# A four-layer Trainium2 kernel: the mixer's filters and first inputs made beside attention 2, its later inputs in steps

## The chip, the cores and the metric

The kernel runs on one core of one Trainium2 chip. A core has five engines that matter here, each working through its own instructions in order: PE (matrix products, with weight loads shown as PEld), DVE (vector operations), ACT (activations), POOL (a second vector engine) and SP (issues DMAs). The engines wait for each other through semaphores. The metric is the device time of one execution in microseconds (us); the time of a kernel is the median of its runs.

## The reference

Everything is float32. The input x has 2 images of 56 x 56 positions (L = 3136) and C = 128 channels. The stages are chained: two layers of selective scans with their convolutions and gates, then attention 2, then the mixer (a spectral layer), attention 3, and a layer of experts. What the change touches is the mixer and the two attentions around it. Attention 2 is self-attention of each position over all others but itself, with a residual. The mixer takes u, the layer-normalized tokens, and computes

```python
# phi: (length, K=16) filters; M_plus, M_minus: (4, K, d, d); sgn = +1, -1, +1, ...
Vf = rfft(phi, n); Uf_p = rfft(u, n); Uf_m = rfft(u * sgn, n)
U_plus = irfft(Vf * Uf_p)[:sl]            # causal convolution of every channel with 16 filters
U_minus = irfft(Vf * Uf_m)[:sl] * sgn
s = sigma ** 0.25
out = einsum('btkd,k,kde->bte', U_plus, s, Mpp) + einsum('btkd,k,kde->bte', U_minus, s, Mpm)
out += sum(shift(u, i) @ Mu[i] for i in range(3))      # the "direct" part
```

The four sets of matrices hold for four stretches of the sequence, weighted by a softmax over log_weights + gumbel.

## The kernel before

**Order of the stages.** `program` (L2179) runs the two scan layers, then inside attention 2's memory `MixerInputs` (L1511) and `Attention2.run` (L1297), then `Attention3.__init__` (L1322), `layer2_mixer` (L1801), attention 3 and the experts. A scheduler that knows dependences orders the instructions of each engine from the order in which the code issues them; on the chip each engine keeps that order. Memory that a pool gives back is waited for by the next pool that gets it.

**Filters.** `mixer_filters` (L1460) runs first in `Attention2.run`. POOL clears P (32 x 1712), a DMA loads the filters of 16 indices and two parities into it, and another stores them to DRAM as `raw`. For four sets A, B, C and D of blocks, DVE makes the filter at seven points (-1, 1, -2, 2, half, 0, inf): the convolution of 4 blocks by 4 blocks is done as 7 products of block polynomials at points, in place of 16. Of these, 88 DVE steps work on 32 partitions; four DMAs store the sets to `win`, and 32 DMAs copy `raw` to `last`, the taps of the last rows. The pool m2f holds all this, and it is given back before attention 2's pools open.

**Attention 2** (`Attend.run`, L1203). Of 14 chunks (2 images by 7) of 448 queries each has 25 key tiles. A key tile is a product sc on PE (L1224), an Exp on ACT into one of six buffers e (L1226), a mask by DVE where keys meet their own queries (L1231), a running total on POOL (L1237), and a product av on PE (L1218). Between the tiles the hook `also(at, j)` makes the mixer's inputs of the chunk before: tokens, channels, blocks (into x, which has 13 blocks of 128 positions of one parity) and the direct part (L1600), which needs `wu`, sums of Mu by the weights. The tail of layer 1 before it (L1034 to L1066) and `Attention2.chunk` (L1281, with L1293 and key_tiles L1433) make the normalized tokens, transposed, in seven steps.

**The mixer** has 32 units: 2 parities of the input (`pin`), 8 pairs of filters (f0), 2 parities of the filter (eo). Units 0 to 15 have pin 0. A unit has four squares; a square makes products at seven points on PE (`product`, L1703), which DVE and ACT evict and interpolate (L1725 to L1739), and POOL completes by two additions (L1741). The squares are T by A (u0), A by A plus T by B in one (u2), C by C (S), D by D (u1). Their results are added (L1761, L1772), and `project` (L1842) multiplies them with matrices and DVE adds to A (L1848). For eo = 0 there is also the `remainder` (L1788). Six PSUM banks hold products. The right sides are windows of `win` (`windows`, L1691 and on, through DMAs on SP).

**Values.** The left sides of the products are the input at the seven points, v["T"], v["A"], v["C"], v["D"]: `Mixer.inputs` (L1630). Their input comes from POOL and ACT (L1643 to L1650), and ten DVE steps make the values (L1655 to L1664), all issued in one go. T and A are made ahead of unit 0 and again at the end of unit 15 (inside `coming`); C and D within units 0 and 16, ahead of the squares that need them. `fetch` (L1624) loads the odd parity of x ahead of unit 15. The first windows of all sets, taps and matrices are loaded in `layer2_mixer` ahead of the loop; `Attention3.__init__` (L1338 to L1351) multiplies its weights into one matrix, on PE, ahead of all of these.

Of the kernel before, what the change touches and what calls it, by code (L numbers as in the profile page):

```python
# [14 lines left out]
F32 = mybir.dt.float32  # L15
# [6 lines left out]
B = 2  # L22
HW = 56
L = HW * HW
C = 128
# [1240 lines left out]
class Attention2:  # L1266
# [30 lines left out]
    def run(self, early, inputs):  # L1297

        k = self.k
        done = early()  # L1300
        with k.pool("a2") as sp, ExitStack() as ctx:
            skip = sp.tile([KT, KT], F32, name="skip")
            k.nc.vector.tensor_scalar(skip, k.ident, -1.0, 1.0, ALU.mult, ALU.add)
            att = Attend(k, ctx)

            def also(at, j):
                steps = {4: inputs.tokens, 11: inputs.channels, 14: inputs.blocks, 18: inputs.direct}
                if at > 0 and j in steps:
                    steps[j](lambda: att.bank("lo"), *divmod(at - 1, NCH))

            att.run(self.uT, self.uT, self.V, 128.0**-0.5, k.ident, skip=skip, also=also)
            for step in (inputs.tokens, inputs.channels, inputs.blocks, inputs.direct):
                step(lambda: att.bank("lo"), B - 1, NCH - 1)
        return done


class Attention3:
# [4 lines left out]
    def __init__(self, k, ctx, d):  # L1322
# [11 lines left out]
        with k.pool("pa3w", psum=True) as pp:  # L1334
            turned = {}
            for n in ("Wq", "Wk"):
                ps = bank(pp, n)[:, 0:C]
                nc.tensor.transpose(ps, W[n], k.ident)  # L1338
                turned[n] = wp.tile([C, C], F32, name=n)
                nc.vector.tensor_copy(turned[n], ps)  # L1340
            ps = bank(pp, "Wq")[:, 0:C]
            nc.tensor.matmul(ps, lhsT=turned["Wq"], rhs=turned["Wk"], start=True, stop=True)
            nc.vector.tensor_copy(self.weights, ps)
            ps = bank(pp, "Wk")[:, 0:1]
            nc.tensor.matmul(ps, lhsT=turned["Wk"], rhs=W["bq"], start=True, stop=False)
            nc.tensor.matmul(ps, lhsT=self.weights, rhs=less[:, 0:1], start=False, stop=True)
            nc.vector.tensor_copy(self.c, ps)
            ps = bank(pp, "Wq")[:TP, 0:C]
            nc.tensor.matmul(ps, lhsT=less, rhs=W["Wv"], start=True, stop=False)
            nc.tensor.matmul(ps, lhsT=k.ones[:, :TP], rhs=W["bv"], start=False, stop=True)  # L1350
            nc.vector.tensor_copy(self.bias, ps)  # L1351
# [102 lines left out]
POINTS = ("-1", "1", "-2", "2", "half", "0", "inf")  # L1454
# [5 lines left out]
def mixer_filters(k, d, dp):  # L1460
# [3 lines left out]
    raw = dp.tile([32, PW], F32, name="raw")  # L1464
    win = dp.tile([32, NWIN, WIDE], F32, name="win")
    last = dp.tile([32, KB, NB + 1, REST], F32, name="last")
    with k.tc.tile_pool(name="m2f", bufs=1) as fp:
        P = fp.tile([32, PW], F32, name="P")
        nc.gpsimd.memset(P, 0.0)
        nc.sync.dma_start(P[:, KB - TP : KB + HL], d["L2_phi"].rearrange("f p m -> (f p) m"))  # L1470
        nc.sync.dma_start(raw, P)
        v = nc.vector
        for g, bases in enumerate(SETS.values()):
            D = fp.tile([32, len(POINTS), WIDE], F32, name=f"D{g % 2}")
            h = [P[:, KB * (bases[0] + i) + 1 : KB * (bases[0] + i) + 1 + WIDE] for i in range(4)]
            if len(bases) > 1:
                both = fp.tile([32, 4, WIDE], F32, name="both")
                for i in range(4):
                    at = KB * (bases[1] + i) + 1
                    v.tensor_tensor(both[:, i], h[i], P[:, at : at + WIDE], ALU.add)  # L1480
                h = [both[:, i] for i in range(4)]
            even, odd = (fp.tile([32, WIDE], F32, name=n) for n in ("even", "odd"))
            for p, (m1, m2) in enumerate(((1 / 9, -1 / 3), (-1 / 60, 1 / 36))):
                v.scalar_tensor_tensor(even, h[2], float(4**p), h[0], ALU.mult, ALU.add)
                v.scalar_tensor_tensor(odd, h[3], float(4**p), h[1], ALU.mult, ALU.add)
                v.tensor_scalar_mul(odd, odd, float(2**p))
                for q, (m, op) in enumerate(((m1, ALU.subtract), (m2, ALU.add))):
                    v.tensor_tensor(D[:, 2 * p + q], even, odd, op)
                    v.tensor_scalar_mul(D[:, 2 * p + q], D[:, 2 * p + q], m)
            v.scalar_tensor_tensor(even, h[1], 0.5, h[0], ALU.mult, ALU.add)  # L1490
            v.scalar_tensor_tensor(odd, h[3], 0.5, h[2], ALU.mult, ALU.add)
            v.scalar_tensor_tensor(even, odd, 0.25, even, ALU.mult, ALU.add)
            v.tensor_scalar_mul(D[:, 4], even, 32 / 45)
            v.tensor_scalar_mul(D[:, 5], h[0], -0.5)
            v.tensor_copy(D[:, 6], h[3])
            nc.sync.dma_start(win[:, len(POINTS) * g : len(POINTS) * (g + 1)], D)
# [4 lines left out]
    return last, win  # L1501


class MixerInputs:
# [6 lines left out]
    def __init__(self, k, ctx, early, d, A, uT):  # L1511
# [44 lines left out]
        mu = ep.tile([128, 4, 3, C], F32, name="mu")  # L1556
        nc.sync.dma_start(mu, d["L2_M_u"].rearrange("i s d e -> d i s e"))
        self.wu = ep.tile([128, 4, 3, C], F32, name="wu")
        stretch_sums(nc.vector, self.wu, mu, lambda i: wt[:, i : i + 1])

# [46 lines left out]
class Mixer:  # L1607
# [5 lines left out]
    def __init__(self, k, ctx, given, last, win):  # L1613
        self.k, self.x, self.odd, self.last, self.win = k, given.x, given.odd, last, win
# [7 lines left out]
        self.W, self.v, self.waiting = {}, {}, []  # L1622
# [7 lines left out]
    def inputs(self, name):  # L1630


        nc, x = self.k.nc, self.x
        n = B * C

        def at(t, i0, m):
            return t[:, i0 : i0 + m]

        if name == "C":
            c = x[:, 4:11]  # L1640
        else:
            c = self.scratch("u0" if name == "D" else "u1", 7)
            if name == "T":  # L1643
                nc.scalar.copy(at(c, 0, 4), x[:, 8:12])
                nc.gpsimd.memset(at(c, 4, 3), 0.0)
            elif name == "A":
                nc.gpsimd.tensor_tensor(c, x[:, 0:7], x[:, 4:11], ALU.subtract)
            else:
                nc.gpsimd.tensor_tensor(at(c, 0, 4), x[:, 8:12], x[:, 4:8], ALU.subtract)
                nc.scalar.activation(at(c, 4, 3), x[:, 8:11], AF.Copy, scale=-1.0)  # L1650
        v = self.sp.tile([KB, len(POINTS), n], F32, name="v" + name)
        e = at(v, 0, 6)
        f, g = self.scratch("T4", 4), self.scratch("T", 2)
        stt, tt = nc.vector.scalar_tensor_tensor, nc.vector.tensor_tensor
        stt(e, at(c, 0, 6), -0.5, at(c, 1, 6), ALU.mult, ALU.add)  # L1655
        stt(f, at(e, 0, 4), -4.0, at(e, 2, 4), ALU.mult, ALU.add)
        tt(g, at(e, 3, 2), at(e, 1, 2), ALU.subtract)
        tt(v[:, 0], f[:, 2], f[:, 1], ALU.subtract)
        tt(v[:, 1], f[:, 2], f[:, 1], ALU.add)
        stt(v[:, 2], g[:, 0], -2.0, g[:, 1], ALU.mult, ALU.add)  # L1660
        stt(v[:, 3], g[:, 0], 2.0, g[:, 1], ALU.mult, ALU.add)
        stt(v[:, 4], c[:, 3], -5.0, c[:, 5], ALU.mult, ALU.add)
        stt(v[:, 4], c[:, 1], 4.0, v[:, 4], ALU.mult, ALU.add)
        tt(at(v, 5, 2), at(f, 2, 2), at(f, 0, 2), ALU.subtract)  # L1664
        self.v[name] = v

    def scratch(self, name, n):
        if name[0] == "T":
            t = self.half(name)
        else:  # L1670
            t = self.block(name)
        t = t.rearrange("p b f c -> p (b f c)")
        return t[:, 0 : n * B * C].rearrange("p (k c) -> p k c", c=B * C)
# [15 lines left out]
    def windows(self, name, f0, eo):  # L1689
        n, n0 = len(POINTS), len(POINTS) * list(SETS).index(name)  # L1690
        t = self.wp.tile([KB, 2, n, KB], F32, name="w" + name)  # L1691
        for f in range(2):
            r = (2 * (f0 + f) + eo) * NWIN + n0
            self.k.nc.sync.dma_start(
                t[:, f], bass.AP(self.win.tensor, self.win.offset + r * WIDE, [[1, KB], [WIDE, n], [1, KB]])
            )
# [12 lines left out]
    def square(self, u, *pairs):  # L1709
# [23 lines left out]
        ps = self.product(4, pairs)  # L1733
        for o, share in ((t(0), -0.25), (t(1), -0.125), (y(2), 1.25), (y(1), 0.625)):
            stt(o, ps, share, o, ALU.mult, ALU.add)  # L1735
        T4 = self.half("T4")
        nc.scalar.activation(T4, T, AF.Copy, scale=4.0)  # L1737
        tt(y(0), self.product(5, pairs), y(2), ALU.add)
        tt(y(3), self.product(6, pairs), y(1), ALU.add)  # L1739
# [3 lines left out]
    def unit(self, f0, eo, after, later, project, ready, coming):  # L1743

        nc = self.k.nc
        u0 = self.block("u0")
        self.square(u0, ("T", "A"))
        self.finish(1)
        u2 = self.block("u2")
# [5 lines left out]
        if ready:  # L1755
            self.inputs("C")
# [468 lines left out]
```

## Time and profile before

| | us |
|---|---|
| median of 3 runs (8737.68, 8746.86, 8752.1) | 8746.86 |
| profiled execution | 8761.79 |
| its span | 8760.0 |
| layers 0 and 1, to the last scan product | 0 to 5532 |
| tail of layer 1 and preparation of attention 2 | 5532 to 5650 |
| filters | 5650 to 5676 |
| attention 2 | 5676 to 6295 |
| mixer | 6295 to 7869 |
| attention 3 | 7869 to 8560 |
| experts, to the end | 8560 to 8760 |

The granted clock is 0.964 in the mean. The profile is one execution on the chip; its times are microseconds from the start of the span. A row of the timeline gives the start, the duration, the engine, the line of the kernel, the operation, the tiles it writes and reads, how many were run in a row (x), and in brackets the idle time of the engine just before, with what ended it. A row of the windows view gives the busy time of each engine within a stretch. A busy time says little by itself: a step matters where another engine that sets the end stands idle for it.

### The profile page before, as it was taken

The page shows a single profiled execution, that of the slowest core. Times are in us where ns is not written, and L with a number is a line of the kernel's source. Part 1 is how long each engine was busy: PE and PEld are TensorE (multiplying, and loading weights), DVE is VectorE, ACT ScalarE, POOL GpSimd, SP SyncE. Part 2 cuts the span into 40 slices and gives each one's busy share as a digit, 9 for nine tenths or more (in the row PEclk, how much of TensorE's full clock was granted, in tenths as well). Part 3 has the DMA queues.
Part 4 walks back from the last instruction along what each step waited for, and adds up shares of the span by engine and source line. Part 5 has one row for each costly group of instructions (what it writes and reads, how often), then busy time and mean ns, then how long its engine had stood idle before and what let it go on. Part 6 is the DMA issues. An engine that isn't in the chain of part 4 may idle for free. (4 is left out here: it accounts for less than half of the span.)

```text
span 8760.0 us, 106320 instructions
## 1 busy us (share of the span) xinstructions
PE 8013.3 (91%) x32199; PEld 4929.5 (56%) x32199; DVE 6642.9 (76%) x6889; ACT 5622.6 (64%) x12956; POOL 6845.1 (78%) x4232
## 2 busy tenths in 40 slices
PE   8999999999998898898888889699899989989998
PEld 4555555555555454445444455355488878865555
DVE  8999998999996997998899799711266676665442
ACT  6888876888876997998898799543322222224330
POOL 5999986999995997998899799566667767756551
PEclk9999999999998999999999999799999999989999
DMA  5666663666663884886788598300133433310004
GB/s 147 217 217 210 211 194 115 217 218 214 211 199 96 228 224 127 218 224 165 183 230 219 130 232 223 80 14 4 47 97 102 116 87 101 102 47 8 15 1 140
DMA packets 846633, 1276.86 MB, mean 146 GB/s; under 512 B 182813, under 2 KB 504350, under 8 KB 846058
## 3 DMA queue, kind: packets, MB, share of 16 engines
q1 hardware_dynamic: 846058, 1270.07, 51.8%
q8 instruction: 254, 4.16, 0.2%
q14 instruction: 321, 2.63, 0.1%
HBM read 1230.00 MB, written 46.58 MB: 146 GB/s over the span
## 5 line engine op out<-in xcount | busy, mean ns | idle before, releaser
L495 POOL TENSOR_TENSOR p<-h,c 128x784 f32<-128x784 f32 x2048 | 3765.8, 1867 | 209.2 <-DVE h L401 114.0
L401 DVE TENSOR_TENSOR_SCAN h<-a,state,h 128x784 f32<-128x784 f32 x1104 | 1993.7, 1834 | 29.5 <-POOL h L498 27.2
L421 PE MATMUL acc<-p,center 128*128 128x392 f32 x4096 | 1482.7, 500 | 24.3 <-POOL p L495 24.2
L421 PE MATMUL acc<-p,ident 128*128 128x392 f32 x4096 | 1427.8, 492 | 0.5 <-POOL p L495 0.4
L479 DVE TENSOR_TENSOR h<-du,b 128x784 f32<-128x784 f32 x1024 | 976.9, 954 | 192.5 <-PE b L407 175.5
L421 PEld LDWEIGHTS acc<-p,center 128*128 128x128 f32 x4096 | 747.6, 192 | 546.6 <-POOL p L495 57.2
L421 PEld LDWEIGHTS acc<-p,ident 128*128 128x128 f32 x4096 | 746.5, 190 | 532.4 <-issue 29.5
L1237 POOL TENSOR_TENSOR total<-total,e 128x448 f32<-128x448 f32 (+1 forms) x644 | 735.6, 1142 | 328.7 <-ACT e L1226 289.4
L1226 ACT ACTIVATE e<-sc 128x448 f32<-128x448 f32 (+1 forms) x700 | 377.5, 543 | 723.2 <-PE sc L1224 594.6
L498 POOL TENSOR_TENSOR h<-du,b 128x784 f32<-128x784 f32 x448 | 832.8, 1859 | 0.0
L381 ACT ACTIVATE a<-delta,L1A 128x784 f32<-128x784 f32 x768 | 700.9, 913 | 148.3 <-DVE h L401 144.2
L401 DVE TENSOR_TENSOR_SCAN h<-h,state,a 128x784 f32<-128x784 f32 x432 | 795.4, 1841 | 0.0
L381 ACT ACTIVATE a<-delta,L0A 128x784 f32<-128x784 f32 x704 | 643.0, 914 | 169.8 <-DVE h L401 164.4
L359 ACT ACTIVATE X<-X,BT 112x128 f32<-112x128 f32 x2100 | 683.7, 390 | 0.2
L401 DVE TENSOR_TENSOR_SCAN h<-a,h 128x784 f32<-128x784 f32 x368 | 644.3, 1775 | 29.5 <-POOL h L498 24.0
L1741 POOL TENSOR_TENSOR u<-u,T 128x1024 f32<-128x1024 f32 x192 | 448.9, 2359 | 264.8 <-DVE u L1739 264.8
L407 PE MATMUL b<-three,sel 96*128 96x512 bf16 (+1 forms) x2048 | 516.1, 333 | 100.2 <-DVE h L479 42.7
L1725 ACT ACTIVATE less<-cv 128x512 f32<-128x512 f32 x256 | 152.2, 595 | 611.5 <-PE cv L1703 586.2
L359 ACT ACTIVATE big<-big,BT 112x64 f32<-112x64 f32 x1680 | 446.4, 336 | 0.0
L359 ACT ACTIVATE pair<-big,BT 112x64 f32<-112x64 f32 x1680 | 444.0, 337 | 0.0
L1737 ACT ACTIVATE T<-T 128x1024 f32<-128x1024 f32 x128 | 135.2, 1056 | 407.5 <-DVE T L1735 279.0
L407 PEld LDWEIGHTS <-sel 96*128 96x128 bf16 x2048 | 198.1, 100 | 319.9 <-issue 214.1
(545 smaller groups left out, 15050.5 us busy)
## 6 DMA issues: line engine op xcount, KB each, us to landing
c<-rows SPq DMA_DIRECT2D x1024, 392.0 KB, 4.0
c<-rows SPq DMA_DIRECT2D x2048, 196.0 KB, 4.6
b<-rows SPq DMA_DIRECT2D x512, 196.0 KB, 4.7
b<-rows SPq DMA_DIRECT2D x192, 392.0 KB, 4.5
wA<-win SPq DMA_DIRECT2D x64, 448.0 KB, 3.9
wB<-win SPq DMA_DIRECT2D x64, 448.0 KB, 6.3
wC<-win SPq DMA_DIRECT2D x64, 448.0 KB, 4.8
wD<-win SPq DMA_DIRECT2D x64, 448.0 KB, 3.8
```

Of the source, the lines that this page charges most:

```text
L359: self.k.nc.scalar.activation(x["bT"][:, i, c0:c1], g["duT"][x["ci"]][:, i, c0:c1], AF.Copy, scale=g["BT"][:, r : r + 1])
L381: self.k.nc.scalar.activation(x["a"], g["delta"][ci], AF.Exp, scale=self.w["A"](g["kd"], ci, x["n"]))
L401: self.k.nc.vector.tensor_tensor_scan(h, a, b, start, ALU.mult, ALU.add)
L407: self.k.nc.tensor.matmul(ps[:, c0:c1], lhsT=self.w["selB"](x["n"]), rhs=x["g"]["three"][:, c0:c1], start=True, stop=True)
L421: nc.tensor.matmul(job["acc"][:, i, 0:392], lhsT=self.w["sum"], rhs=x["p"][:, 392 * i : 392 * (i + 1)], start=False, stop=n == NS - 1,)
L479: nc.vector.tensor_tensor(one["h"], one["g"]["du"][one["ci"]], one["b"], ALU.mult)
L495: nc.gpsimd.tensor_tensor(now["p"], now["h"], now["c"], ALU.mult)
L498: nc.gpsimd.tensor_tensor(three["h"], three["g"]["du"][three["ci"]], three["b"], ALU.mult)
L1226: nc.scalar.activation(e[:n], ps[:n], AF.Exp, scale=scale)
L1237: nc.gpsimd.tensor_tensor(total[:n], total[:n], e[:n], ALU.add)
L1725: nc.scalar.activation(turned, self.product(2 * j, pairs), AF.Copy, scale=float(1 + j))
L1741: nc.gpsimd.tensor_tensor(u[:, :, :, o], u[:, :, :, o], half, ALU.add)
```

## The change

Five parts:

1. `mixer_filters` becomes a generator, which stops after each DVE step. Its tiles are now views of tiles that the mixer uses later (vT, vC and the first window wA, in the pool mixx, which lies apart from attention 2's). `Attention2.run` starts it by `given.filters` and calls `inputs.step()` from the hook `also`, twice per key tile in the first image and once in the second. The `last` DMAs are issued right after `raw`, ahead of the filters' stores.
2. The values T and C of unit 0 are steps from key tile 20 of the third and the fifth chunk of the second image, on the hook; the first window wA is loaded at the start of the second image.
3. The values A and D of unit 0, and those of T, A, C and D for pin 1 (in units 15 and 16), are issued a step at a time between the evictions of a square, with `need` making what is left before a square uses it.
4. Attention 3's preparation is a method, called in unit 4 (`coming`), with banks of `pproj`.
5. The points are ordered with "half" last, and products are indexed to match; the first windows, taps and matrices are issued as B, matrices, C, taps, D.

```diff
 class Attention2:
-    def run(self, early, inputs):
+    def run(self, inputs):
         k = self.k
-        done = early()
...
             def also(at, j):
...
+                if j == 20 and at - 1 in (NCH + 2, NCH + 4):
+                    inputs.early("T" if at - 1 == NCH + 2 else "C")
+                if at == NCH and j == 0:
+                    inputs.first_window()
+                for _ in range(2 if at < NCH else 1):
+                    inputs.step()
...
-def mixer_filters(k, d, dp):
+def mixer_filters(k, d, raw, win, last, P, D, rest):
...
     for f in range(32):
         nc.sync.dma_start(
             last[f], bass.AP(raw.tensor, raw.offset + f * PW + 1, [[1, KB], [KB, NB + 1], [1, REST]])
         )
-    return last, win
+    yield
+    v = nc.vector
+    for g, bases in enumerate(SETS.values()):
...
+        for p, (m1, m2) in enumerate(((1 / 9, -1 / 3), (-1 / 60, 1 / 36))):
+            v.scalar_tensor_tensor(even, h[2], float(4**p), h[0], ALU.mult, ALU.add)
+            yield
...
+def values(nc, x, name, v, c):
...
+    elif name == "A":
+        nc.gpsimd.tensor_tensor(c, at(x, 0, 7), at(x, 4, 7), ALU.subtract)
+        yield
+    else:
+        nc.gpsimd.tensor_tensor(at(c, 0, 4), at(x, 8, 4), at(x, 4, 4), ALU.subtract)
+        nc.scalar.activation(at(c, 4, 3), at(x, 8, 3), AF.Copy, scale=-1.0)
+        yield
+    stt, tt = nc.vector.scalar_tensor_tensor, nc.vector.tensor_tensor
+    e, f, g = at(v, 0, 6), at(c, 0, 4), at(c, 4, 2)
+    stt(e, at(a, 0, 6), -0.5, at(a, 1, 6), ALU.mult, ALU.add)
+    yield
+    stt(v[:, 6], a[:, 3], -5.0, a[:, 5], ALU.mult, ALU.add)
+    yield
...
 class Mixer:
+    def step(self):
+        while self.todo and next(self.todo[0][1], self) is self:
+            self.todo.pop(0)
+    def need(self, *names):
+        while any(name in names for name, _ in self.todo):
+            self.step()
...
     def square(self, u, *pairs):
...
+            self.step()
+            self.step()
-        ps = self.product(4, pairs)
+        ps = self.product(6, pairs)
         for o, share in ((t(0), -0.25), (t(1), -0.125), (y(2), 1.25), (y(1), 0.625)):
             stt(o, ps, share, o, ALU.mult, ALU.add)
+            self.step()
...
-    def unit(self, f0, eo, after, later, project, ready, coming):
+    def unit(self, f0, eo, after, later, project, state, coming):
+        self.need("T")
+        if state == "first":
+            self.inputs("A", "u1")
+        elif state == "second":
+            self.inputs("C", "S")
         u0 = self.block("u0")
         self.square(u0, ("T", "A"))
         self.finish(1)
+        self.need("A")
+        if state == "first":
+            self.inputs("D", "u1")
         u2 = self.block("u2")
         self.square(u2, ("A", "A"), ("T", "B"))
...
         self.finish()
-        if ready:
-            self.inputs("C")
+        self.need("C")
+        if state == "last":
+            self.inputs("T", "u1")
+        elif state == "second":
+            self.inputs("D", "u1")
         S = self.block("S")
         self.square(S, ("C", "C"))
...
-        if ready:
-            self.inputs("D")
+        self.need("T", "D")
+        if state == "last":
+            self.inputs("A", "u0")
         u1 = self.block("u1")
         self.square(u1, ("D", "D"))
...
 def layer2_mixer(k, d, given, aside):
...
+        mixer.windows("B", 0, 0)
+        Ws = [matrices(f) for f in range(2)]
+        mixer.windows("C", 0, 0)
         for eo in range(2):
             mixer.taps(0, eo)
-        for name in SETS:
-            mixer.windows(name, 0, 0)
-        mixer.inputs("T")
-        mixer.inputs("A")
-        Ws = [matrices(f) for f in range(2)]
+        mixer.windows("D", 0, 0)
...
                 if eo == 1 and n + 1 < len(units):
-                    if f0 == NF - 2:
-                        mixer.inputs("T")
-                        mixer.inputs("A")
                     given.extend(matrices((f0 + 2) % NF + f) for f in range(2))
+                if n == 4:
+                    aside(lambda: p2.tile([128, 512], F32, name="pj"))
...
-                (f0, eo) == (0, 0), coming,
+                {0: "first", len(units) // 2 - 1: "last", len(units) // 2: "second"}.get(n), coming,
```

The states "first", "last" and "second" are units 0, 15 and 16.

## The prediction

> **What bounds the kernel now.** I read the page first. Its busy line has PE at 91% of the span, and its part of 40 slices has PE at 9 or 8 tenths nearly everywhere. A step on DVE, ACT, POOL or SP then costs only where PE stands still for it, so I cut the trace into stages and looked for such places near the change. First the busy line, then the windows view (columns: stretch, length, then PE, PEld, DVE, ACT and POOL busy with their counts, granted clock, DMA share, GB/s):
>
> ```profile
> PE 8013.3 (91%) x32199; PEld 4929.5 (56%) x32199; DVE 6642.9 (76%) x6889; ACT 5622.6 (64%) x12956; POOL 6845.1 (78%) x4232
> ```
>
> ```profile
> 5532.00:5650.00 118.00, 67.22 (x325) 45.70 (x324) 79.95 (x139) 66.40 (x174) 48.31 (x32) 0.66 0.01 3
> 5650.00:5676.00 26.00, 0.00 (x0) 0.00 (x0) 23.92 (x84) 0.58 (x1) 0.10 (x1) 0.50 0.67 114
> 5676.00:6295.00 619.00, 609.04 (x1846) 315.64 (x1846) 113.00 (x265) 242.36 (x433) 397.79 (x350) 0.98 0.07 12
> 6295.00:6383.00 88.00, 55.24 (x230) 46.75 (x230) 58.78 (x84) 18.79 (x37) 51.58 (x37) 0.75 0.50 132
> 6383.00:7005.00 622.00, 622.00 (x3109) 538.84 (x3108) 406.49 (x673) 150.08 (x231) 450.28 (x210) 1.00 0.39 107
> 7005.00:7135.00 130.00, 99.76 (x449) 82.79 (x448) 98.30 (x138) 23.04 (x35) 79.23 (x34) 0.88 0.27 74
> ```
>
> The rows are: the tail of layer 1; the filters; attention 2; unit 0; units 1 to 14; units 15 and 16. PE is full in the third and fifth. It stands still in the second, and partly in the fourth and the sixth. Next the timeline of ACT and PE at the second row (start, us, what, idle before with its releaser):
>
> ```profile
> 5675.42 1.28 ACT L1226 ACT_TABLE_LOAD   x1 [25.45 <-DVE odd L1491]
> ...
> 5677.31 1.86 PE L1224 MATMUL sc<-big 128*128 128x448 f32 x2 [28.29 <-ACT e L1226]
> ```
>
> Attention 2's first Exp waits for a DVE step of the filters, because its tiles lie where the filters' did, and PE waits 28.29 for the Exp. Last, rows of PE, DVE and POOL in the mixer, those of unit 0 and one of unit 16:
>
> ```profile
> 6306.26 8.86 PE L1703 MATMUL cv<-wA,vT 128*128 128x256 f32 x28 [3.33 <-DMA wA<-win]
> ...
> 6351.24 8.56 PE L1703 MATMUL cv<-wC,vC 128*128 128x256 f32 x28 [11.46 <-issue]
> ...
> 6368.03 5.53 POOL L1761 TENSOR_TENSOR u<-u,S 128x2048 f32<-128x2048 f32 x1
> ...
> 6369.24 4.60 DVE L1658 TENSOR_TENSOR vD<-T 128x256 f32<-128x256 f32 x1
> ...
> 6373.90 9.19 PE L1703 MATMUL cv<-wD,vD 128*128 128x256 f32 x28 [8.29 <-DVE vD L1658]
> 6382.92 6.21 PE L1703 MATMUL cv<-wA,vT 128*128 128x256 f32 x28
> ...
> 7124.99 2.08 PE L1842 MATMUL pj<-u,Wm 128*128 128x512 f32 x2 [9.12 <-POOL u L1761]
> ```
>
> PE stops for values DVE has yet to make. L1658 took 4.60 beside a POOL row of 5.53 that ends with it, and its neighbours at L1659 to L1662 took 0.41: DVE and POOL hold each other up when both read SBUF.
>
> **The change part by part.** All is summed against the profiled execution: 8761.8 (span 8760.0), 14.9 above the median 8746.9 of the three runs.
>
> *Filters off the path.* The stall of 28.29 goes: -28. The work remains: 88 DVE steps that took 24.3 from 5651.8 to 5676.1, 0.28 each. By the order of instructions of the changed kernel some 43 stand among the tail's DVE steps and some 45 in chunk 0 of attention 2. The tail's share is 12 us, and DVE is idle there 118 - 80 = 38. So 0 is one end. The other is 12, for the tail is a chain over PE, DVE, ACT and POOL and each step may delay it. I take +3, near 0, since most steps stand behind waits for other engines, and the routing steps of L1534 to L1555 with the sums of L1888 and L1890 (5528 to 5540), which headed the tail, now come later. The first filter step waits for the DMA of P: POOL's memset (1.52) comes behind its last scan product (5532.1) and the DMA lands 2.6 later, at 5536.3; the tail's first DVE step ran at 5540.6, so nothing is late. Two more ACT table loads (Exp begins before the tail's last roots) are 2 x 1.28 on ACT, not all on the path: +1. In chunk 0 the 45 steps are 13 us of DVE, idle there for about 506 of 619. What they can hold is POOL: one total takes 1.13 of each 1.50 per key tile. Ends 0 and 13; six e buffers let POOL fall some 6 us behind, so +2. The mixer sums' DMA now stands on SP behind P, raw, 32 `last` issues (1.33 each in a row of three, 43 us) and the first two window stores; POOL's memset for T waits on these sums, with totals queued behind it. Ten totals into chunk 0 it is within the same 6 us. Sum of this part: -22.
>
> *T and C during image 2.* These are 2 x 10 DVE steps, 6.3 each set by the vA rows from 6309.71 to 6316. They stand in bunches beside totals, with 0.37 of POOL idle per tile: ends 0 and 13, taken +3.
>
> *Mixer start.* The last direct product ends at T0 = 6295.2. Unit 1 starts at 6382.9, 87.7 later; PE's own work in unit 0 is 39.6 (12.1 for the double square, 6.05 for each of three products' sets (216 ns by 28), 3.5 project, 5.9 remainder). So 48 is lost, the end of what can be won; 0 is the other. In the changed order the first product waits for nothing new: T0. POOL makes A's input by T0+4.3 (3.96 by L1647), DVE makes vA between the T/A evictions (6.3 + 6) by T0+17, the double square ends about T0+29. POOL then has the matrices, two additions of u0 (5.02 in a row) and D's input (2.4), to about T0+31. vD stands in DVE's queue ahead of the double square's last evictions and waits for that input; with PE's six banks full, PE waits too. Those evictions end near T0+50. What follows (product of C, project, remainder, product of D: 21.6, 2 overlapped) gives unit 1 at T0+69.5: -18. This is nearer to the low end, because one queue is still served in order.
>
> *Attention 3's preparation* (L1338 to L1351) leaves the start (in the -18) and comes in unit 4, where PE was full. Its PE rows from 6297.11 to 6302.93 hold 4.1 and its waits for copies 3.7: ends 4 and 8, taken +4.
>
> *Middle.* Units 15 and 16 took 129.6; a steady pair takes 41.5 + 47.4 = 88.9. So 41 is lost, which is the end; 0 the other. DVE was busy 74.1 of the 95 us from 7040 to 7135 and idle for 21. Four value sets are 25 of that. With steps between evictions the order lets DVE run from unit 15's S square (about 7034), but the same work and the same holds of POOL remain: 67 + 19 = 86, unit 17 at about 7120 instead of 7134.8. So -16 is taken, nearer to what DVE's idle time allows than to PE's.
>
> *Points in another order, windows by another function:* the same counts and durations, 0.
>
> Sum: -22 + 3 - 18 + 4 - 16 = -49. Profiled time 8713; median 8746.9 - 49 = **8698**.
>
> **A rule against the change.** The Trainium skill (SBUF — State Buffer, Who interferes with whom) says that a VectorE instruction with two SBUF inputs and a GpSimd instruction that reads SBUF exclude each other, the later one waiting for the earlier to end. The rows at 6368 agree (4.60 for 0.41). By that rule every two-input step put beside POOL's totals (1.13) could wait up to 1.13, 88 x 1.13 = 99 us of DVE, estimated from the page's rule. It would turn the sum only if DVE ended last there.
>
> **The rivals.** (a) *Only the filters' part pays*: the two bursts of the mixer are DVE and POOL work that steps only rearrange. For it: DVE is busy 74 of 95 in the middle, and vD still waits for POOL ahead of evictions. Then -22 + 3 + 4 - 8 (the preparation out of the start) = -23: 8724. (b) *All stalls vanish*, PE being full all through: -28 - 48 - 41 + 4 = -113: 8634. For it: DVE's work per unit is 31 of 41.5, so a spread set fits within a few units; against: the sets are still due within one unit. (c) *Slower*: the filters' steps in the layer-1 tail are held by POOL instructions (1.51 mean there, 48.31 over 32) and delay the in-order DVE queue, on which each L64 copy feeds PE. Place: 43 steps; price: 43 x (0.28 + 1.51) = 77 on the chain, chunk 0 hiding its own. Net -28 + 77 + 1 + 2 + 3 - 18 + 4 - 16 = +25: 8772. It decides from 43 steps at about 1.2 us each on (52 us). Against: in that tail two-input rows such as L1051 take their usual 0.41; for: L1534 took 3.72 at 5528.36. (d) *The change does not do what it says*: the scheduler may keep a late DMA or memory reuse ahead of the first Exp, so that the stall only moves. Then the filters give 0 and the two bursts little: 8742. Against: the first steps of attention 2 in the changed order wait for no filter.
>
> **How the numbers follow.** Forecast (-30 to -75) 0.56; (a) 0.20; (b) 0.11; (c) 0.07; (d) 0.06. The range of 8 in 10 takes the forecast, most of (a) and the near part of (b): 8655 to 8733. A measurement of this kernel tells about 0.2%, 17.5 us, from no change. Faster by more: the forecast, (b) and most of (a), 0.85; within: (d) and the rest of (a), 0.08; slower: 0.07.
>
> **What would show it.** In the profile after, the first L1224 products after the tail should have no idle time over 5 us where 28.29 stood; the tail from the last scan to the first L1249 should be 22 us nearer. From the last direct product to unit 1 the trace should show 70 (88 before), and units 15 and 16 together 114 (130). The step at vD should be a DVE row waiting for POOL, with PE idle behind it. Held filter steps above 1.2 us in the tail would prove (c); unit 0 under 55 would prove (b). Wrong would be, above all, my contention of 19 in the middle and the vD wait in unit 0, both of which come from the order and not from a measured row.

## The result, and the profile after

The changed kernel took 8694.99 us (median of 4 runs, 8691.8 to 8705.03), the kernel before 8742.27 beside it: a ratio of 0.9941, with a 95% interval of 0.993 to 0.9953. On another chip it was 8708.97 against 8760.43, ratio 0.9939 (0.9925 to 0.9952). The forecast for the median was 49 us less; 47 and 51 were measured.

The busy line of the changed kernel, and its windows view with cuts at the same places of the work as before (tail of layer 1, attention 2, unit 0, units 1 to 14, units 15 and 16):

```profile
PE 8000.5 (92%) x32199; PEld 4919.9 (57%) x32199; DVE 6671.3 (77%) x6889; ACT 5624.9 (65%) x12958; POOL 6857.9 (79%) x4232
```

```profile
5522.00:5652.00 130.00, 73.95 (x336) 48.67 (x336) 105.61 (x199) 73.51 (x182) 58.38 (x39) 0.69 0.41 66
5652.00:6264.00 612.00, 603.35 (x1837) 313.15 (x1836) 151.56 (x308) 239.87 (x428) 397.45 (x346) 0.99 0.02 6
6264.00:6328.00 64.00, 46.53 (x219) 39.50 (x218) 41.95 (x60) 18.71 (x37) 52.49 (x36) 0.84 0.62 166
6328.00:6952.00 624.00, 624.00 (x3122) 540.50 (x3121) 408.12 (x678) 149.81 (x231) 451.13 (x210) 1.00 0.39 107
6952.00:7066.00 114.00, 97.08 (x444) 80.63 (x443) 96.38 (x133) 23.04 (x35) 77.58 (x33) 0.93 0.30 83
```

The row of 26 us in which PE did nothing is gone. The tail grew from 118 to 130, and DVE is busy 105.61 in it, where it was 79.95. Attention 2 carries 151.56 of DVE in place of 113.00. Unit 0 shrank from 88 to 64 and units 15 and 16 from 130 to 114.

One profile against another hides a spread: the end of the last scan product lay between 5520.6 and 5544.6 us in the profiles of this study, though the scans' instructions stand in the same order; here it was 5532.1 before and 5522.1 after. So all that follows compares stages between events within one run. For one kernel (changed and a1) these repeat to a few tenths in the mixer and attention 2, and to some 4 us in the tail. Between kernels, a stage that an edit does not touch can still move by up to 1.7 (units 15 to 17 of e3, e4 and e5, where the same steps are issued as in the changed kernel), so less than 2 us in that column is not read as an effect.

| kernel | last scan product to T0 | first chunk's end to unit 1 | T0 to unit 1 | unit 4 | units 15 to 17 |
|---|---|---|---|---|---|
| before | 763.1 | 664.9 | 87.7 | 47.4 | 170.3 |
| changed | 742.1 | 640.6 | 63.5 | 49.0 | 156.6 |
| a1 (changed again) | 746.4 | 640.2 | 63.3 | 49.0 | 156.6 |
| e1 filters at once | 742.8 | 640.3 | 63.3 | 49.0 | 156.6 |
| e2 values at once | 742.1 | 630.9 | 53.8 | 49.0 | 162.1 |
| e3 T, C in the mixer | 741.7 | 650.6 | 73.2 | 49.0 | 154.9 |
| e4 preparation at the start | 746.4 | 640.9 | 63.7 | 47.4 | 157.8 |
| e5 D early | 743.3 | 631.1 | 49.7 | 49.0 | 157.8 |
| e7 filters only | 742.1 | 647.5 | 70.1 | 47.4 | 160.6 |
| e8 the same, old scratch | 742.1 | 648.7 | 71.2 | 47.4 | 162.1 |
| e9 D early, A at once | 747.0 | 634.3 | 49.6 | 49.0 | 156.5 |
| e10 unit 0 at once | 742.2 | 631.5 | 54.0 | 49.0 | 156.5 |
| e11 filters only, old places | 742.2 | 658.9 | 81.8 | 47.4 | 166.5 |
| e12 the same, old loads | 742.1 | 658.7 | 81.6 | 47.3 | 164.9 |

T0 is the end of the last direct product. The first chunk's end is the start of its first product at L1253, the transposes of its output. A unit starts with its first product of wA by vT; units 15 to 17 are taken as three, from the start of 15 to that of 18, since work is pushed from 16 into 17. The second column holds attention 2 from its first chunk on as well as unit 0, so it also shows what work made early costs there. Between before and changed the columns differ by -21.0 (first), -24.2 (third), +1.6 (unit 4) and -13.7 (last), -57.3 together (-53 with a1's columns); the end of the kernel adds +2.1 and the scans' spread the rest of the two profiles' difference of 65. The medians say 47 and 51, from runs of one kernel that lie up to 21 us apart. So by the stages the change is worth some 4 to 8 us more than the forecast, and that 47 lies so near to 49 is in part luck.

### The profile page after: what moved, and what is told of

Same layout as the page of the kernel before. It is cut to its first block, busy times and chain, and to the rows that moved or that the text cites. A ratio compares the mean times of both kernels' runs of the same rounds, so it can differ in the third digit from the quotient of the medians.

```text
span 8695.0 us, 106299 instructions
## 1 busy us (share of the span) xinstructions
PE 8000.5 (92%) x32199; PEld 4919.9 (57%) x32199; DVE 6671.3 (77%) x6889; ACT 5624.9 (65%) x12958; POOL 6857.9 (79%) x4232
## 5 line engine op out<-in xcount | busy, mean ns | idle before, releaser
L421 PEld LDWEIGHTS acc<-p,center 128*128 128x128 f32 x4096 | 741.7, 191 | 541.1 <-POOL p L495 57.4
```

The lines of the kernel that those rows point to most:

```text
L421: nc.tensor.matmul(job["acc"][:, i, 0:392], lhsT=self.w["sum"], rhs=x["p"][:, 392 * i : 392 * (i + 1)], start=False, stop=n == NS - 1,)
```

## The experiments

**Filters at once (e1).** The generator is run to its end ahead of attention 2.

```diff
-        self.todo = [mixer_filters(...)]
+        for _ in mixer_filters(...):
+            pass
+        self.todo = []
```

> The changed kernel, but the filters' generator is run to its end at one place, ahead of attention 2 (with its tiles in the same memory of their own, and the scheduler free to place the steps). Stage watched: from the end of the last scan product to the last direct product T0 (763.1 before, 742.1 changed). Theory 'memory': attention 2 waited because its tiles lay where the filters' did, so the new place of the tiles is the gain, and this stage stays within 2 us of 742.1. Rival 'steps': the 24 us of DVE steps ahead of the attention's tiles hold DVE, and taking them apart is the gain: the stage is longer by 10 to 24, 752 to 766.

Measured: 742.8. The theory "memory" holds: what kept the first Exp waiting was that its tiles took the filters' place, and issuing the steps one by one from the hook adds nothing to that. The scheduler mixes them into the tail by itself: 62 of the 84 steps ran there, 60 in the changed kernel. So on the chip they did not stand in a row here either, and no run has them in a row with tiles of their own. The changed kernel's PE timeline at the join shows the new state (14 av products in a row are seven key tiles, whose sc products had run within the tail):

```profile
5651.43 1.12 PE L1439 MATMUL pt<-ident,big 128*128 128x128 f32 x4 [0.62 <-ACT big L68]
5652.34 7.19 PE L1218 MATMUL av<-e,big 128*128 128x448 f32 x14
```

**Filters only (e7).** Of the change only the filters' part, the points' order and the new issue places stay: values at once, T and C in the mixer, the preparation at the start.

```diff
-        self.todo.append((name, values(self.k.nc, self.x, name, self.v[name], c)))
+        for _ in values(self.k.nc, self.x, name, self.v[name], c):
+            pass
...
-                if j == 20 and at - 1 in (NCH + 2, NCH + 4):
-                    inputs.early("T" if at - 1 == NCH + 2 else "C")
...
+        aside(lambda: p2.tile([128, 512], F32, name="pj"))
         mixer.windows("B", 0, 0)
...
+        mixer.inputs("T", "u1")
```

> Of the change only the filters' part and the order of points stay: T at once ahead of unit 0, A, C and D at once within it, values of units 15 and 16 at once, attention 3's preparation at the start of the mixer. Theory 'parts add': last scan product to T0 within 2 us of 742.1; T0 to unit 1 between 80 and 92 (87.7 before); unit 15 to unit 17 between 122 and 132; unit 4 without the 1.6 more than steady. Rival 'the filters' part lives off T and C being early' (as their tiles and order meet in attention 2): last scan product to T0 differs from 742.1 by over 4.

The first stage is 742.1: the parts add there. But T0 to unit 1 is 70.1 and units 15 to 17 take 160.6, better than before by 17.6 and 9.7 without a single step of the values. (I had put units 15 and 16 between 122 and 132; they took 119.1.) Something that I had costed at nothing was doing this.

**Values at once (e2).** Steps undone in the mixer, T and C still early.

```diff
-        self.todo.append((name, values(self.k.nc, self.x, name, self.v[name], c)))
+        for _ in values(self.k.nc, self.x, name, self.v[name], c):
+            pass
```

> The changed kernel, but the values that the mixer makes itself (A and D of unit 0; T, A, C, D in units 15 and 16) are issued all eleven steps in one go, at the place where the changed kernel begins to step them. Stages watched: T0 to unit 1 (87.7 before, 63.5 changed) and unit 15 to unit 17 (129.6 before, 114.3 changed). Theory 'steps let DVE's idle time be used': PE's banks fill while DVE makes a set, some 6 us for each set: T0 to unit 1 about 70 (two sets, partly beside waits for POOL), units 15 and 16 about 128 (four sets). Rival 'only the earlier places count': both within 3 us of the changed kernel.

Both theories miss in unit 0: it gets better by 9.7 (53.8), of which 0.8 is given back in unit 1 (42.3 for 41.5). They miss in units 15 and 16 too, which took 120.6, between the 128 of the one and the 114 of the other; over units 15 to 17 the steps are worth 5.5 (162.1 to 156.6). In the changed kernel's unit 0, rows of PE, then of POOL, then of DVE:

```profile
6277.64 1.19 PE L1770 MATMUL cv<-wA,vA 128*128 128x256 f32 x2 [7.32 <-ACT mpm L1905]
...
6297.70 2.08 PE L1770 MATMUL cv<-wC,vC 128*128 128x256 f32 x4 [5.46 <-DVE u L1796]
6300.87 2.04 PE L1770 MATMUL cv<-wC,vC 128*128 128x256 f32 x4 [1.09 <-DVE T L1799]
6306.51 6.02 PE L1770 MATMUL cv<-wC,vC 128*128 128x256 f32 x16 [3.60 <-DVE u L1804]
```

```profile
6264.49 3.98 POOL L1532 TENSOR_TENSOR u<-x 128x1792 f32<-128x1792 f32 x1
...
6287.18 4.67 POOL L1813 TENSOR_TENSOR u<-u,T 128x1024 f32<-128x1024 f32 x2
6291.81 2.34 POOL L1535 TENSOR_TENSOR u<-x 128x1024 f32<-128x1024 f32 x1
```

```profile
6280.70 1.75 DVE L1558 TENSOR_TENSOR vA<-u 128x512 f32<-128x512 f32 x1
6294.18 2.27 DVE L1540 SCALAR_TENSOR_TENSOR vD<-u 128x1536 f32<-128x1536 f32 x1 [11.73 <-POOL u L1535]
```

D's input (L1535) uses the block of A's input and so waits for A's last step. A's steps, one by one between evictions, end only at 6282.4, and by then POOL's matrices and the additions of u0 stand ahead of it: it is done 30 us after T0. DVE waits 11.73 at vD, the double square's evictions queue behind vD, and PE's banks are full. The PE row that ends the idle 7.32 names an ACT operation, but it is the first product with vA, and the first points of vA were done just then (6277.5); the same row of e10, below, has DVE's vA as its releaser. In e10's unit 0 (the same as e2's), POOL and PE:

```profile
6279.68 3.98 POOL L1532 TENSOR_TENSOR u<-x 128x1792 f32<-128x1792 f32 x1
6291.15 2.37 POOL L1535 TENSOR_TENSOR u<-x 128x1024 f32<-128x1024 f32 x1 [7.49 <-DVE vA L1558]
```

```profile
6289.54 1.19 PE L1770 MATMUL cv<-wA,vA 128*128 128x256 f32 x2 [4.03 <-DVE vA L1550]
...
6311.55 1.02 PE L1929 MATMUL pj<-u,Wm 128*128 128x196 f32 x2 [4.96 <-POOL u L1813]
```

With A made in one go, D's input is POOL's next instruction. It is done 14 us after T0, ahead of the matrices.

**T and C in the mixer (e3).**

```diff
-                if j == 20 and at - 1 in (NCH + 2, NCH + 4):
-                    inputs.early("T" if at - 1 == NCH + 2 else "C")
...
+        mixer.inputs("T", "u1")
+        mixer.need("T")
```

> The changed kernel, but T of unit 0 is made at once at the head of the mixer and C in steps in its second square (D in its third); the filters, the steps, attention 3's preparation in unit 4 stay. Theory 'T and C early shorten the start': T0 to unit 1 goes from 63.5 to 74 or more (T's 6.3 on the path ahead of the first product, C's steps among the evictions that already bound PE). Rival 'DVE's idle time takes them': 63 to 68. The last scan product to T0 stays at 742 if T and C beside attention 2 cost nothing, as the changed kernel's chunks (43.2 each) suggest.

73.2 and 741.7: T and C early are worth 9.7 (10.0 in the column from the first chunk's end), close to the 74 of the first theory. Beside attention 2 they cost nothing: first chunk's end to T0 is 577.4 here and 577.1 changed.

**Preparation at the start (e4).**

```diff
-                if n == 4:
-                    aside(lambda: p2.tile([128, 512], F32, name="pj"))
...
+        aside(lambda: p2.tile([128, 512], F32, name="pj"))
         mixer.windows("B", 0, 0)
```

> The changed kernel with attention 3's preparation ahead of the first product, as before the change. Theory 'it is on the path at the start': T0 to unit 1 longer by 4 to 8 (63.5 to 68 to 72), unit 4 back from 49.0 to 47.4. Rival 'it is hidden there, since PE waits for A's values anyway (7.32 idle)': T0 to unit 1 within 2 us of 63.5 and the whole 1.6 shorter than the changed kernel.

The rival holds: 63.7, and unit 4 is back at 47.4. Moving the preparation gained nothing and cost 1.6. The first column's 746.4 is no part of it: a1, the changed kernel again, has 746.4 too.

**Old scratch (e8).** e7, with the values' intermediate results in the squares' T4 and T again.

```diff
-    e, f, g = at(v, 0, 6), at(c, 0, 4), at(c, 4, 2)
+    e = at(v, 0, 6)          # f, g: tiles T4 and T, as before
```

> The kernel of e7_filters_only (T0 to unit 1 70.1, units 15 to 17 160.6, against 87.7 and 170.3 before), with one thing more undone: the intermediate values f and g lie again in the squares' own tiles T4 and T, as before the change, and not in the tile of the input. Theory 'shared scratch': before, DVE's value steps waited for POOL's additions that still read T and T4 (8.54 and 4.54 in unit 0, 3.36, 4.16 and 2.23 in units 15 and 16), and that is what e7 gained without any steps: T0 to unit 1 goes back to 82 or more, units 15 to 17 to 167 or more. Rival 'the order of the first loads and of POOL's matrices': both stay within 4 us of e7.

My theory falls: 71.2 and 162.1, only 1.1 and 1.5 more. The waits of 8.54 and 4.54 for POOL's additions were real, but at the new issue places they are not on the path.

**Old places, and old loads (e11, e12).** e7 with the value sets issued where the kernel before had them. For C and D of unit 0, and for T and D of pin 1, that is one square later, for C of pin 1 two; A of pin 1 comes a little earlier. D's input also lies in the block u0 again. e12 also has the first loads and matrices in the old order.

```diff
-        elif state == "second":
-            self.inputs("C", "S")            # ahead of the square T by A
...
+        if state in ("first", "second"):
+            self.inputs("C", "S")            # ahead of S
         S = self.block("S")
...
+        if state in ("first", "second"):
+            self.inputs("D", "u0")           # ahead of the square D by D
```

> The kernel of e7_filters_only, but the value sets are issued where the kernel before issued them: T and A ahead of unit 15's projection, C ahead of S, D ahead of the last square. (e7 has each set one square earlier.) Theory 'the earlier place is what e7 gained in the middle': units 15 to 17 go from 160.6 back to 166 to 171 (170.3 before), and T0 to unit 1 from 70.1 to 76 or more. Rival 'the place is nothing, the scheduler moves the steps anyway': both within 3 us of e7.

> The kernel of e11_old_places, and the first loads too in the order of before: taps, windows, T and A, and only then the matrices. Left of the change are the filters' part, the order of points and the intermediate values in the input's tile. Theory 'POOL's matrices ahead of the values, and the loads' order, made the rest of what e7 gained in unit 0': T0 to unit 1 goes to 83 to 90 (87.7 before), units 15 to 17 stay where e11 has them. Rival: within 3 us of e11.

The place theory holds: from the first chunk's end to unit 1 it is 11.4 (647.5 to 658.9; 0.8 of it comes back in unit 1), in units 15 to 17 5.9 (160.6 to 166.5). The order of the loads is nothing (e12 658.7 and 164.9, less than 2 from e11), so its theory falls. e11's unit 0 shows what a late D costs, on PE, DVE and POOL:

```profile
6332.55 2.08 PE L1914 MATMUL pj<-u,Wm 128*128 128x512 f32 x2 [14.23 <-POOL u L1832]
...
6337.20 8.25 PE L1769 MATMUL cv<-wD,vD 128*128 128x256 f32 x28 [2.58 <-issue]
```

```profile
6328.08 6.03 DVE L1538 SCALAR_TENSOR_TENSOR vD<-u 128x1536 f32<-128x1536 f32 x1 [5.86 <-POOL u L1533]
```

```profile
6321.10 4.65 POOL L1812 TENSOR_TENSOR S<-S,T 128x1024 f32<-128x1024 f32 x2 [1.60 <-DVE S L1809]
6325.71 2.34 POOL L1533 TENSOR_TENSOR u<-x 128x1024 f32<-128x1024 f32 x1
6328.01 4.49 POOL L1832 TENSOR_TENSOR u<-u,S 128x2048 f32<-128x2048 f32 x1
```

D's input comes behind the additions of S on POOL and ahead of the addition at L1832, for which PE stands idle for 14.23. Beside that addition vD's first step takes 6.03 (1.76 for the same step of vA in e10), and PE waits 2.58 more ahead of D's products. With each set issued earlier (e7) PE's idle time of over 0.3 us at a stretch in unit 0 is 18.3 in sum, here 29.0.

**D early (e5, e9).** D of unit 0 is made beside attention 2 too.

```diff
+                if j == 8 and at - 1 == NCH + 5:
+                    inputs.early("D")
...
-        by = self.ep.tile([128, CH], F32, name="by")       # two buffers
+        by = self.by.tile([128, CH], F32, name="by")       # one
```

> The changed kernel, with D of unit 0 made during attention 2's last chunk as well (vD in the pool of vT and vC; room for it is made by a single buffer for the tile by). Stage watched: T0 to unit 1 (63.5 changed). In the changed kernel DVE waits 11.73 for POOL's input of D ahead of the double square's evictions. Theory 'that wait is on the path': it goes, and 11 to 14 with it: 50 to 53, and the whole about 0.15 % shorter than the changed kernel (8682). Rival 'PE is held by A's values and POOL's additions anyway': 60 or more.

> The changed kernel with D of unit 0 made in attention 2's last chunk (behind its start, by a one-element copy that D's input must wait for, so that no mask queues behind it), and A of unit 0 made at once; units 15 and 16 keep the steps. Theory 'in unit 0 the steps hold A back': T0 to unit 1 goes from 49.7 (e5_D_early) to 42 to 47, near PE's 39.6; the first chunk's end to T0 is 577 again (581.4 in e5). Together some 18 to 22 us less than the changed kernel. Rival 'with D gone, A in steps costs nothing': 49 to 51.

e9 also holds D's input back by a copy of one element, so that no mask queues behind D, and makes A at once.

In e5, T0 to unit 1 is 49.7, so the wait was on the path; 8687.92 (8686.41 to 8691.11), ratio to before 0.992 (0.9903 to 0.9936). But attention 2 pays: from the first chunk's end to T0 581.4 in place of 577.1, all of it in the chunk in which D's steps ran, the last but one (47.9 for 42.9). Unit 1 takes 1.1 more. e9 expected the cost in attention 2 gone and A at once to gain; the first got worse (584.7; the last chunk took 50.2 for 42.3), and A at once gains nothing once D is out (49.6). The whole was 8693.55 (8678.68 to 8696.32). PE and DVE rows of e5, then of e9:

```profile
6201.95 1.02 PE L1219 MATMUL av<-e,big 128*128 128x448 f32 x2 [1.28 <-DVE e L1232]
6205.55 1.02 PE L1219 MATMUL av<-e,big 128*128 128x448 f32 x2 [1.83 <-DVE e L1232]
6208.42 1.02 PE L1219 MATMUL av<-e,big 128*128 128x448 f32 x2 [1.10 <-DVE e L1232]
```

```profile
6200.06 1.83 DVE L1232 TENSOR_TENSOR e<-e,skip 128x128 f32<-128x128 f32 x1 [0.74 <-ACT e L1227]
...
6206.55 1.62 DVE L1551 TENSOR_TENSOR mu<-vD 128x512 f32<-128x512 f32 x1
6208.09 0.28 DVE L1232 TENSOR_TENSOR e<-e,skip 128x128 f32<-128x128 f32 x1
```

```profile
6242.24 1.13 PE L1683 MATMUL lo<-ident,pair 128*128 128x128 f32 x4 [6.16 <-DVE pair L1673]
```

```profile
6240.05 1.61 DVE L1561 TENSOR_TENSOR vD<-mu 128x512 f32<-128x512 f32 x1
6241.58 0.61 DVE L1673 COPY pair<-lo 128x448 f32<-128x448 f32 x1
```

In e5 two of the masks (L1232) queue behind D's steps, and the one before them takes 1.83 for 0.28 beside POOL's input of D. In e9 no mask comes behind D, but the copy of `pair` does, for ten steps beside POOL's totals took 1.24 to 2.67 each.

**Unit 0 at once (e10), beside the changed kernel (a1).**

```diff
             self.inputs("A", "u1")
+            self.need("A")
...
             self.inputs("D", "u1")
+            self.need("D")
```

> The changed kernel, but A and D of unit 0 are made at once, where the changed kernel begins to step them; units 15 and 16 keep the steps. Theory 'the steps help where four sets meet in 100 us, and hurt in unit 0, where D's input on POOL waits until A's last step': T0 to unit 1 54 (as in e2_values_at_once), units 15 to 17 156.6 (as in the changed kernel), the whole 8 to 11 us less than a1. Rival 'the gain in unit 0 is given back in the units after': the whole within 3 us of a1.

> The changed kernel itself, beside the other three on one chip. All reasons expect its own numbers: last scan product to T0 742, T0 to unit 1 63.5, units 15 to 17 156.6, a median 45 to 65 below that of the kernel before.

As expected: 54.0 and 156.5, with 0.7 given back in unit 1 (42.2 for 41.5). On one chip e10 took 8692.13 (8686.88 to 8702.27; ratio to before 0.9925, 0.9912 to 0.9937) and a1 8708.97 (8697.3 to 8718.24). Of the 16.8 between these medians the mixer's start explains 9.3; 4.2 more lie between the last scan product and T0, where a1 and the changed kernel differ by as much among themselves. The two kernels' times overlap in part, so it is the stages that tell them apart: from the first chunk's end to the start of unit 2, e10 takes some 8 us less than the changed kernel, and e5 the same.

## Why the prediction was right, point by point

**Filters: -22 forecast, -21.0 measured** (-16.7 in a1). The stall was the right term, but two sizes beside it were off and cancelled. The tail was to grow by 4 (steps and table loads); its last transpose product ended 116.9 after the last scan product before and 130.4 in the changed kernel: +13.5, some of it products of attention 2 that PE now makes there. In return the first av product comes no later than that, 30.2 gone, and the first chunk, to which 2 was charged, takes 34.8 in place of 39.0: seven key tiles wait ready. I had 43 steps in the tail and 45 in chunk 0 by the listing; 60 and 24 ran there. They are 84, and not the 88 that I counted from the code. The rows of the changed kernel for some of them, by line, from the tail (busy us, then mean ns):

```profile
L1499 DVE TENSOR_TENSOR vC<-wA 32x255 f32<-32x255 f32 x12 | 4.5, 403 | 0.0
L1488 DVE TENSOR_TENSOR wA<-vT 32x255 f32<-32x255 f32 x4 | 3.2, 793 | 0.0
L1503 DVE SCALAR_TENSOR_TENSOR wA<-vT 32x255 f32<-32x255 f32 x2 | 3.0, 1480 | 0.0
```

All 60 took 27.7 (0.46 each), the 24 of chunk 0 15.5 (0.65), where the same 84 took 28.0 before. So they were held, 15.2 in sum, and far less than 1.2 each, from which rival (c) decided. Single steps were held that long: five of the 60 in the tail took over 1.2, one at L1503 2.56 beside a POOL row of 2.41, where no filter step took over 0.42 before. I had called that a proof of (c), and it was none, for the tail grew by 13.5 and not by 77. Of the 14 that took over 1 us, five read only one input. Most steps were not held at all: 59 of the 84 start while POOL is between two instructions or waits itself. The Trainium skill (SBUF — State Buffer, Who interferes with whom) says that a VectorE instruction with two SBUF inputs contends with a GpSimd instruction that reads SBUF. The trace agrees with the kind of that lock, and not with the 99 us that I had estimated from it as the most it could cost.

**T and C beside attention 2: +3 forecast, 0 measured** (577.2 and 577.1). With D there too it was 4.3 in e5 and 7.6 in e9. Whether that is the third set as such, or its place among the masks and copies of the last chunks, no run parts.

**Mixer start: -18 forecast, -24.2 measured, and for other reasons in part.** The vD wait was there as I had read it from the order (11.73 on DVE for POOL's input of D, done at T0+30 where I had T0+31). The term that was mis-sized in that chain is the end of the double square's evictions: T0+50 by my sum, T0+42 in the trace (the PE row at 6306.51). What failed is the step that named the gain: "DVE makes vA between the T/A evictions" was to be part of what is won, and it is a loss, of 9.5 (e2, e10). What won was T and C early (9.7 with the steps, e3; with values at once e2 against e7 gives 16.6, the preparation's share of which e4 shows to be nothing in the stepped kernel) and the issue of the sets earlier (11.4, e7 against e11). The last was in the diff, and I had not made a term of it. It is also why rival (a), "steps only rearrange", did not come: it spoke of steps, and the place matters more. From before to e11 are 6.0 that no run parts further (the first window loaded early, the points' order, the scratch). Together, in the column from the first chunk's end: 6.0 + 11.4 + 16.6 - 9.7 = 24.3.

**The preparation: +4 forecast, +1.6 measured**, and its absence at the start is worth nothing (e4). The 4 was the length of its rows at the start; in unit 4 they run among other products, and PE is not idle ahead of any of them.

**Middle: -16 forecast, -15.3 measured for units 15 and 16**, and 1.6 given back in unit 17. The reason given, that steps let DVE's idle time be used, is right for the smaller part: steps 4.0 to 5.5 (e7, e2), the earlier place 5.9 (e11), what is left 3.8 (166.5 to 170.3). The idle time of PE ahead of D's products in unit 16 did not go, it shrank. Before, it was 9.12, ended by POOL's addition at L1761, beside which a step of vD took 4.98 in place of 0.68:

```profile
7120.51 4.98 DVE L1657 TENSOR_TENSOR T<-vD 128x512 f32<-128x512 f32 x1
```

In the changed kernel it is 2.17, for vD itself, the last of these rows:

```profile
7006.81 3.78 PE L1927 MATMUL pj<-u,Wm 128*128 128x512 f32 x4 [6.82 <-POOL u L1844]
...
7030.66 0.70 PE L1770 MATMUL cv<-wA,vA 128*128 128x256 f32 x2 [4.16 <-DVE u L1804]
...
7057.98 8.26 PE L1770 MATMUL cv<-wD,vD 128*128 128x256 f32 x28 [2.17 <-DVE vD L1550]
```

The other two rows are where the time still goes: an addition on POOL, and evictions behind the values. So the number was right with one term well founded (the stall), two beside it whose sizes cancelled (the tail and the first chunk), and two, the start and the middle, that came out within some 6 of their size for a mechanism that was mine in part only.

## What to carry to other kernels

When work is taken apart into steps and also issued earlier, cost the two apart: here the earlier place gave as much as the steps or more, and in one place the steps cost 9.5 us (some 8 with what comes back in the next unit), because the next link of the chain (an input on another engine) waited for the last step and lost its place in that engine's queue. Where an engine stands idle ahead of a stage, look first at whose memory the stage waits for: giving the early work tiles of its own took the whole stall away, whether it was issued in steps or in one go. Work hidden beside another stage stays free only until something on the same in-order queue, a mask or a copy, comes behind it.

## What was not expected of the hardware

The end of the scans, some 5500 us of the same instructions in the same order, came between 5520.6 and 5544.6 us from run to run. That spread of 24 us is half of what was to be measured, while a steady unit of the mixer repeats to 0.1 (41.5 and 47.4 in all profiles). Stages within one run told terms of 2 us apart that whole times could not.
